# Self attention with 8-bit rounding: an input's scalings spread over two turns, new weights rounded behind the exponentials, output weights left unscaled

## The chip, the cores and the metric

One core of a Trainium2 chip runs the whole program. The metric is the device time of one execution in microseconds (us). Five runs of the kernel before gave a median of 3887.34 us (3884.24 to 3895.66). An engine is one of TensorE (PE, with its weight loads PEld), VectorE (DVE), ScalarE (ACT), GpSimd (POOL) and SyncE (SP, which here only issues DMAs). Each engine runs its own list of instructions in order; a semaphore holds an instruction until what it needs is done.

## What is computed

A decoder of two layers on 16 batches of 112 positions and 512 features. The change touches the second of its seven stages, the self-attention half of the first layer's mixed attention, and in one point the third, its cross-attention half. Cut to what matters:

```python
ln_out = _ln(hidden_states, ln_w, ln_b)
q = _ln(_fp8_linear_pertensor(ln_out, wq, wq_scale, q_in_scale).reshape(b, s, g, hpg, d), qln_w, qln_b)
k = _ln(_fp8_linear_pertensor(ln_out, wk, wk_scale, k_in_scale).reshape(b, s, g, d), kln_w, kln_b)
v = _fp8_linear_pertensor(ln_out, wv, wv_scale, v_in_scale).reshape(b, s, g, d)
core = _gqa(q, k, v).reshape(b, s, nh * d)
...
cat = jnp.concatenate([core, xout], axis=-1)
catq = _div_clamp_fp8(cat, proj_smooth)
return jnp.einsum('bsi,oi->bso', catq, wproj) * (proj_in_scale * proj_w_scale)
```

`_fp8_linear_pertensor` divides its input by a scale for each feature, rounds it to an 8-bit float and multiplies by the weights and both scales. The result of the last line is added to `x`.

## The kernel before

**Stages.** Seven stages follow each other. The first attends over the batch positions (up to about 290 us in the profile), the second is `stage_fp8_self` (L915, to about 960 us), the third `stage_fp8_cross` (to about 2310 us); then come a mixture of experts, another self attention, another cross attention and a feed-forward part.

**Units and turns.** The self stage has four head groups q of four heads each, and 16 batches. A unit (`SelfUnit`) is one (q, batch); `self_order` (L902) lists the 64 units: the eight batches 0 to 7 of q = 0 are units 0 to 7, then batches of q = 0 and q = 1 are mixed until unit 31, then q = 2 and q = 3 follow. The 16 x 112 rows make 14 tiles of 128 rows, so batches 7 and 15 have no tile of their own, and their units no query product. `turn(n)` (L956) runs n from -2 and works on several units at once: the query product, key and value products, and normalization of unit n; transposes of its normalized queries and keys one turn later; scores, minimum (`su_m`) and exponentials (`pr`) of unit n - 2; transposed probabilities (`pt`) and values (`ps_av`) of unit n - 3, followed by their division and rounding (`r_y`, `r_o`); the output product and its addition to `x` for unit n - 4. TensorE, ACT and, from turn 5 on, DVE run in exactly the order in which the code is written (`manual_schedule`, L1009 and L1012). POOL and SP are ordered by the scheduler's own estimate; it is fixed once the program is built.

**Inputs.** A unit of q = 0 with a tile makes its own input (`Quantized`): the normalized rows `xn` are loaded one turn ahead, transposed on TensorE into one PSUM bank (`ps_xt`), and scaled by ACT into 16 pieces `y` of 128 x 128, eight for queries and keys, four for values, four for the later cross stage (L695). `round_qk` and `round_v` round the first eight and the next four with `round_fp8`: four steps on DVE (L504 to L508) and a subtraction on POOL (L510), which writes `xq` or `xv`. Copies go to DRAM, from where the other head groups load them. In the kernel before, turn n does all of this for the input of unit n + 2. These inputs belong to units 0 to 6, 8, 10, 12, 15, 17, 19 and 22, so turns -2 to 4, 6, 8, 10, 13, 15, 17 and 20 carry one.

**Weights.** Each head group's weights arrive in 12 chunks of 128 x 512 (`raw`, two buffers), split by `Weights.part` (L597) into a rounded part `hi` and a remainder `lo`, so that two matmuls make one product (`two_parts`). Six chunks of the query and key weights are centered on DVE first (L587 to L594, at the end of the turn that loads them); at the start of the next turn `ends` runs: ACT casts to `hi` (L617), POOL subtracts (L618). Chunks that aren't centered, two of values and four of the output, are first scaled by ACT in place (L616), the values by the input's scales, the output by the one number `c_proj`. From turn 3 two chunks a turn are prepared for q = 1, from turn 24 two a turn for q = 2, from turn 31 one a turn for q = 3, and from turn 47 one a turn for the cross stage, which goes on in the same way itself.

**Statistics.** `project_kv` (L776) squares queries and keys on ACT (L761), sums on DVE (L764, `su_v`), and calls `rsqrt`, two POOL instructions (L491 and L492). `normalize` multiplies the products by it on DVE (L804, `qk`), which also frees their PSUM banks: the three banks `mm` hold query products (`ps_q`) and key and value products (`ps_kv`) in turn, the four banks `sc` hold scores, transposes, values and the output product.

**Early products.** In turns -2 to 4 TensorE also computes 16 key products of the cross stage (`ps_early`).

**Addition.** `add_output` (L894), called for each tile and head group by both the self and the cross stage, multiplies `r_o` by the output weights and adds the PSUM bank to `x` on DVE (L899).

## Time and profile before

| what | value |
| --- | --- |
| median of 5 runs | 3887.34 us (3884.24 to 3895.66) |
| the profiled execution's own time | 3887.62 us |
| its span, first to last instruction | 3885.9 us |
| mean granted clock of TensorE | 0.968 |
| TensorE busy, share of the span | 94% |
| VectorE, ScalarE, GpSimd | 45%, 38%, 24% |
| the 16 scalings of an input (L695), x224 | 537 ns mean of one, issued 0.37 us apart |
| cast of a chunk (L617), x48 and x32 | 619 and 618 ns (median) |
| scaling of an output chunk (L616), x32 | 731 ns (median) |
| scaling of half a value chunk (L616), x16 | 524 ns (median) |
| subtraction of a chunk on POOL (L618), x48 and x32 | 1286 and 1270 ns (median) |

The page gives busy time of each engine and the clock that the throttle granted. The span can be cut into stretches and busy time, clock and DMA share read for each; the table of waits says for which line an engine stood still and what released it, with the sum, the number and the longest; the timeline lists instructions in order of time with the idle time before them in brackets.

### The profile page before, as it was taken

To read this page: it belongs to the slowest core of one execution; us is meant where nothing else is said; L and a number is where in the kernel's file an instruction comes from. 1 tells how busy PE (TensorE), PEld (TensorE's weight loads), DVE (VectorE), ACT (ScalarE), POOL (GpSimd) and SP (SyncE) were. 2 spreads that over 40 slices of the span, in tenths; PEclk is the share of its full clock that TensorE was granted. 3 is DMA by queue.
4 is the path that set the end of the run, shared out by engine and by line. 5 is a ranking of instruction groups with operands and counts; after the bars stand their busy time and mean duration, and the time that the engine had idled before them with its cause. 6 is when DMAs were issued, how large, how long until landed. Compare 5 with 4: busy or idle time off the path is not lost.

```text
span 3885.9 us, 46312 instructions
## 1 busy us (share of the span) xinstructions
PE 3642.9 (94%) x16482; PEld 2353.8 (61%) x16482; DVE 1759.4 (45%) x3856; ACT 1462.5 (38%) x4189; POOL 935.1 (24%) x1322
## 2 busy tenths in 40 slices
PE   7888889999899999999999999999889989999999
PEld 4445778887555565666666654555444445556788
DVE  4445767775554544544445543111333343214333
ACT  2556666555544444444444430111123341112222
POOL 2333545554322322222222210000222220000000
PEclk8999889999999999999999999999989999999999
DMA  2125323442211211211121114999820013122000
GB/s 74 56 89 180 106 86 118 132 136 73 84 55 51 76 48 46 70 51 51 48 76 49 43 46 140 320 314 320 292 94 12 1 47 104 64 79 82 11 12 17
DMA packets 118118, 364.56 MB, mean 94 GB/s; under 512 B 13281, under 2 KB 33249, under 8 KB 108849
## 3 DMA queue, kind: packets, MB, share of 16 engines
q1 hardware_dynamic: 105504, 332.20, 26.5%
q0 software_dynamic: 5040, 16.52, 1.2%
q10 hardware_dynamic: 7344, 12.89, 0.9%
q8 instruction: 131, 2.15, 0.2%
q14 instruction: 99, 0.80, 0.1%
HBM read 317.09 MB, written 44.47 MB: 93 GB/s over the span
## 4 chain that ended last, share of the span: by engine, by line
PE 72%; DVE 7%; ACT 3%; issue 3%; POOL 3%; DMA 2%; SPq 0%; ACTq 0%; POOLq 0%; DVEq 0%
PE ps_kv L1081 14%; PE ps L1430 5%; PE ps_acc L664 4%; PE ps_q L664 4%; PE ps_av L1134 4%; PE ps_s L1109 3%; PE ps_y L1448 3%; PE ps_u L1785 3%; PE ps_o L341 3%; PE ps_o L1767 3%; PE ps_q L1536 3%; PE ps_g L1785 3%; PE ps_p L1629 3%; PE ps_pt L1124 2%; PE ps_kv L664 2%
## 5 line engine op out<-in xcount | busy, mean ns | idle before, releaser
L1081 PE MATMUL ps_kv<-w_kv,ct 128*125 128x512 f32 x1408 | 638.4, 593 | 0.0
L1081 PEld LDWEIGHTS ps_kv<-w_kv,ct 128*125 128x125 f32 x1408 | 261.4, 188 | 277.2 <-issue 242.0
L510 POOL TENSOR_TENSOR r_o<-r_t,r_m 128x64 fp32r<-128x64 bf16 (+6 forms) x224 | 146.6, 672 | 393.8 <-DVE r_t L508 369.7
L1025 ACT ACTIVATE pr<-ps_s,ex_m 112x375 f32<-112x375 f32 (+1 forms) x272 | 157.4, 579 | 161.1 <-DVE ex_m L1024 150.9
L1430 PE MATMUL ps<-w_expert,xgt 128*128 128x448 f32 x560 | 216.4, 539 | 0.7 <-ACT xgt L1422 0.7
L1057 DVE TENSOR_REDUCE cu_v<-sq 125x2 f32<-125x256 f32 (+1 forms) x248 | 118.6, 478 | 179.7 <-ACT sq L1056 179.5
L233 POOL TENSOR_TENSOR pr<-pr,nq_s 112x448 f32<-112x448 f32 (+1 forms) x120 | 119.4, 996 | 324.5 <-DVE nq_s L232 249.9
L492 POOL TENSOR_TENSOR cu_v<-cu_v,mhalf 125x2 f32<-125x2 f32 (+1 forms) x248 | 190.0, 766 | 20.6
L228 ACT ACTIVATE pr<-ps_s,nq_m 112x112 f32<-112x112 f32 (+1 forms) x480 | 167.3, 373 | 59.2 <-DVE nq_m L220 54.7
L491 POOL TENSOR_SCALAR cu_v<-cu_v 125x2 f32<-125x2 f32 (+1 forms) x248 | 48.0, 194 | 578.4 <-DVE cu_v L1057 575.7
L1109 PE MATMUL ps_s<-kt,qt 128*112 128x375 f32 x512 | 183.1, 479 | 1.4 <-ACT pr L1025 0.9
L1024 DVE TENSOR_REDUCE ex_m<-ps_s 112x1 f32<-112x375 f32 (+1 forms) x272 | 148.4, 545 | 69.1 <-PE ps_s L1656 67.5
L1056 ACT ACTIVATE sq<-ps_kv 125x256 f32<-125x256 f32 x176 | 67.4, 383 | 274.1 <-PE ps_kv L1081 221.5
L485 ACT ACTIVATE qt<-ps_t,turned 128x448 f32<-128x448 f32 (+6 forms) x224 | 116.3, 580 | 137.9 <-PE ps_t L1093 126.5
L1134 PE MATMUL ps_av<-pt,vn 125*128 125x224 f32 x768 | 163.3, 363 | 0.0
L1430 PEld LDWEIGHTS ps<-w_expert,xgt 128*128 128x128 f32 x560 | 103.6, 190 | 92.0 <-issue 91.0
L1124 PEld LDWEIGHTS ps_pt<-ident,pr 112*125 112x125 f32 x768 | 104.3, 191 | 89.1 <-DVE pr L1116 49.8
L242 ACT COPY ptt<-ps_pt 112x448 f32<-112x448 f32 (+1 forms) x120 | 67.3, 561 | 227.6 <-PE ps_pt L240 227.6
L1134 PEld LDWEIGHTS ps_av<-pt,vn 125*128 125x128 f32 x768 | 146.2, 195 | 8.6 <-ACT pt L1127 3.8
L1109 PEld LDWEIGHTS ps_s<-kt,qt 128*112 128x112 f32 x512 | 90.1, 177 | 99.9 <-issue 59.3
L1124 PE MATMUL ps_pt<-ident,pr 112*125 112x112 f32 x768 | 120.1, 287 | 31.5 <-DVE pr L1116 29.5
L485 ACT ACTIVATE kt<-ps_t,vec 128x375 f32<-128x375 f32 (+7 forms) x240 | 131.2, 587 | 26.6 <-PE ps_t L1099 22.5
(294 smaller groups left out, 7425.1 us busy)
## 6 DMA issues: line engine op xcount, KB each, us to landing
w_expert<-in_moe_w SPq DMA_DIRECT2D x105, 896.0 KB
ct<-in_ctx_t SPq DMA_DIRECT2D x64, 750.0 KB
xq<-xq_dram SPq DMA_DIRECT2D x42, 512.0 KB
xq<-xx_dram SPq DMA_DIRECT2D x56, 256.0 KB
raw<-in_self_w SPq DMA_DIRECT2D x48, 256.0 KB
w_sum<-in_ffn_w SPq DMA_DIRECT2D x12, 1024.0 KB
cn<-in_ctx SPq DMA_DIRECT2D x16, 750.0 KB
xv<-xv_dram SPq DMA_DIRECT2D x48, 224.0 KB
```

The source lines that it names most:

```text
L228: nc.scalar.activation(pr[:, j, :], self.ps[:, j, r * t : (r + 1) * t], AF.Exp, bias=self.mx[r][:, j : j + 1], scale=-1.0, accum_out=sums[ ...
L485: k.nc.scalar.activation(dst, src, AF.Identity, bias=cols[:, 1:2], scale=cols[:, 0:1])
L492: nc.gpsimd.tensor_tensor(dst, dst, bc(k.minus_half[: dst.shape[0]], [dst.shape[0], n]), ALU.pow)
L664: k.nc.tensor.matmul(out, lhs(c), w[i][:, c, :], start=first and c == 0 and i == 0, stop=last and c == n - 1 and i == 1,)
L1024: nc.vector.tensor_reduce(mx, src, AX.X, ALU.min)
L1025: nc.scalar.activation(dst, src, AF.Exp, bias=mx, scale=-1.0, accum_out=sums)
L1081: nc.tensor.matmul(pkv, self.ct[:, c, ch * CC : (ch + 1) * CC], w[:, c, :], start=c == 0, stop=c == KC - 1,)
L1109: nc.tensor.matmul(ps, self.heads.qt[self.b][:, h, :], self.kt[:, h // 2, :], start=True, stop=True)
L1124: nc.tensor.transpose(ps[:, h, :], self.pr[:, h, ch * CC : (ch + 1) * CC], k.ident[:S, :S])
L1134: nc.tensor.matmul(av[:, 2 * g : 2 * g + 2, :], self.vn[:, ch, g, :], self.pt[:, ch, 2 * g : 2 * g + 2, :], start=ch == 0, stop=ch == NCH - 1,
L1430: nc.tensor.matmul(pp, self.xt[:, c, :], w[:, c, :], start=c == 0, stop=c == 3)
L1785: nc.tensor.matmul(pp, w[:, c, cols], xt[:, part, c, :], start=c == 0 and part == 0, stop=c == 3 and part == 1,)
```

## The change

Three things are edited, all below.

First, an input is worked on over two turns. `new` is still the input of unit n + 2, but in turn n it is now only transposed and scaled ten times, at the turn's end. `half` is the input of unit n + 1: behind the exponentials its queries and keys are rounded, and six more scalings follow; its values are rounded behind the normalization. `xq` of unit n + 1 is thus made in turn n instead of turn n - 1.

Second, `ends` of all weights moves from the start of the turn to behind the exponentials. For the value weights the scaling and the cast become one ACT instruction for each 256 columns, and the remainder is made on DVE by `scalar_tensor_tensor` (raw times scale, minus `hi`) instead of on POOL.

Third, output weights are no longer scaled. Their factor `c_proj` goes into the addition, which becomes a `scalar_tensor_tensor` (product times `c_proj`, plus `x`), in the self and in the cross stage.

```diff
-        col = lambda i: k.c_proj if scale is None else k.w_cols[:, scale + i : scale + i + 1]
+        col = lambda i: k.w_cols[:, scale + i : scale + i + 1]
...
         def end():
             hi, lo = self.hi[n][:, cols], self.lo[n][:, cols]
-            if not centered:
-                for i in rows:
-                    part = raw[:, i * width - first : (i + 1) * width - first]
-                    nc.scalar.activation(part, part, AF.Copy, scale=col(i))
-            nc.scalar.copy(hi, raw)
-            nc.gpsimd.tensor_tensor(lo, raw, hi.bitcast(F32), ALU.subtract)
+            if centered or scale is None:
+                nc.scalar.copy(hi, raw)
+                nc.gpsimd.tensor_tensor(lo, raw, hi.bitcast(F32), ALU.subtract)
+                return
+            for i in rows:
+                part = slice(i * width - first, (i + 1) * width - first)
+                nc.scalar.activation(hi[:, part], raw[:, part], AF.Copy, scale=col(i))
+                nc.vector.scalar_tensor_tensor(
+                    lo[:, part], raw[:, part], col(i), hi[:, part].bitcast(F32),
+                    ALU.mult, ALU.subtract,
+                )
...
     two_parts(k, acc, lambda h: o[:, h, :], w)
-    k.nc.vector.tensor_tensor(k.x[:, t, :], k.x[:, t, :], acc, ALU.add)
+    x = k.x[:, t, :]
+    k.nc.vector.scalar_tensor_tensor(x, acc, k.c_proj, x, ALU.mult, ALU.add)
...
         def turn(n):
-            new = inputs.get(n + 2)
-            for w in weights:
-                w.ends()
+            new, half = inputs.get(n + 2), inputs.get(n + 1)
             products(early.get(n, 0))
...
             if at(n):
                 units[n].query_sums()
-            if new:
-                new.transpose()
             if at(n - 3):
                 units[n - 3].transpose_probs()
             if at(n - 2):
                 units[n - 2].exponentials()
-            if new:
-                new.scale(5)
+            if half:
+                half.round_qk()
+                xq[n + 1] = half.xq
+            for w in weights:
+                w.ends()
+            if half:
+                half.scale(6)
             if at(n):
                 units[n].project_kv(xv[order[n][0]].pop(order[n][1]))
             for w, count, pieces in due(n):
                 w.begin(count, pieces)
-            if new:
-                new.scale(5)
-                new.round_qk()
             if at(n - 3):
                 units[n - 3].values()
             if at(n):
                 units[n].normalize()
+            if half:
+                half.round_v()
             if at(n - 1):
                 units[n - 1].transpose()
             if at(n - 4):
                 units[n - 4].output()
             if new:
-                new.scale(6)
-                new.round_v()
-                xq[n + 2] = new.xq
+                new.transpose()
+                new.scale(10)
             elif at(n + 2):
```

## The prediction

> **What bounds the kernel now.** The page's first part and the clock row come first, then a table by stretches, cut where the stages and the kinds of turn change (columns: stretch; its us; busy us and instructions of PE, weight loads, DVE, ACT, POOL; granted clock; DMA share; GB/s).
>
> ```profile
> PE 3642.9 (94%) x16482; PEld 2353.8 (61%) x16482; DVE 1759.4 (45%) x3856; ACT 1462.5 (38%) x4189; POOL 935.1 (24%) x1322
> PEclk8999889999999999999999999999989999999999
> ```
>
> ```profile
> 300.00:380.00 80.00, 77.71 (x324) 48.40 (x324) 52.22 (x94) 51.71 (x154) 32.16 (x31) 0.98 0.54 180
> 380.00:429.00 49.00, 31.49 (x142) 26.52 (x142) 36.48 (x74) 31.00 (x93) 27.26 (x29) 0.72 0.34 110
> 452.00:476.00 24.00, 20.95 (x119) 18.47 (x118) 17.14 (x39) 15.53 (x51) 12.90 (x15) 0.86 0.33 113
> 600.00:640.00 40.00, 31.44 (x195) 27.62 (x194) 30.61 (x65) 20.83 (x69) 21.88 (x22) 0.96 0.34 103
> 960.00:2310.00 1350.00, 1310.33 (x4981) 816.04 (x4980) 673.95 (x1622) 598.06 (x1425) 346.37 (x646) 0.99 0.18 57
> ```
>
> TensorE sets the time nearly everywhere. The changed stage, about 290 to 960 us, is the exception: from 380 to 640 TensorE idles and its clock drops, and no other engine is full there, so chains of waits between engines rule. Until 380 the early key products cover everything. The cross stage (960 to 2310) is 97% TensorE. The waits of TensorE in 280:530, then one pair of turns of an input from the timeline, name the chain:
>
> ```profile
> PE ps_kv L664 <- DVE qk L804: 14.2, 5, 4.0
> PE ps_av L858 <- ACT pt L852: 10.2, 3, 5.2
> PE ps_s L826 <- ACT kt L485: 7.2, 5, 3.9
> ```
>
> ```profile
> 456.68 0.36 ACT L839 ACTIVATE pr<-ps_s,su_m 112x112 f32<-112x112 f32 x1
> ...
> 460.23 1.94 ACT L695 ACTIVATE y<-ps_xt,q_bias,q_gain 128x128 bf16<-128x128 f32 x5
> ...
> 463.72 2.12 POOL L510 TENSOR_TENSOR xq<-r_t,r_m 128x1024 fp32r<-128x1024 bf16 x1 [1.28 <-PE ps_q L664]
> 464.15 1.82 DVE L504 TENSOR_SCALAR r_y<-r_y 128x448 bf16<-128x448 bf16 x1
> ...
> 467.68 2.07 PE L664 MATMUL ps_kv<-w_self,xq 128*128 128x256 f32 x8 [2.70 <-DVE qk L804]
> ```
>
> Turn 10 starts at 452.57 (its ps_q), turn 11 at 461.19, turn 12 at 475.46: 22.9 us for a pair whose first turn scales an input. DVE runs in a fixed order, and its four rounding steps stand ahead of the normalization, so they wait for ACT's eighth scaling; then r_y (0.28 elsewhere) lies 1.82 beside POOL's xq. The keys of turn 11 wait for that, and the next 16 matmuls take 3.78 instead of 1.88, at half clock.
>
> The second kind of turn prepares weights (here two chunks a turn):
>
> ```profile
> 617.27 0.61 DVE L832 TENSOR_REDUCE su_m<-ps_s 112x4 f32<-112x448 f32 x1
> 617.38 0.62 ACT L617 CAST w_self<-raw 128x512 fp32r<-128x512 f32 x1 [1.92 <-DVE raw L594]
> 618.08 1.27 POOL L618 TENSOR_TENSOR w_self<-raw,w_self 128x512 fp32r<-128x512 f32 x1 [1.27 <-ACT w_self L617]
> 618.40 0.52 ACT L852 COPY pt<-ps_pt 112x448 f32<-112x448 f32 x1
> 618.81 0.37 ACT L839 ACTIVATE pr<-ps_s,su_m 112x112 f32<-112x112 f32 x1
> 618.97 1.03 PE L858 MATMUL ps_av<-pt,v 112*128 112x224 f32 x4 [3.85 <-ACT pt L852]
> ...
> 621.53 0.20 POOL L491 TENSOR_SCALAR su_v<-su_v 128x6 f32<-128x6 f32 x1
> ...
> 629.78 0.62 DVE L832 TENSOR_REDUCE su_m<-ps_s 112x4 f32<-112x448 f32 x1
> ```
>
> The visible wait is TensorE on pt, behind the cast, behind DVE's centering. But the turn's length, 12.5 us, is a ring: su_m, exponentials, squares of the keys, su_v on POOL, normalization, centering, su_m. Removing the visible wait doesn't shorten the ring.
>
> **Part 1, scalings over two turns.** The 16 scalings are all still there (1.87 for five, 0.37 each), as are the rounding steps. Ten scalings now stand at a turn's end; the query rounding stands behind the next turn's exponentials, six scalings follow, the value rounding stands behind the normalization. In the built program POOL does pr, xq, su_v in the second turn (before: pr, su_v, xq), so su_v queues behind 2.1 us of xq. Recomputed for turns 11 and 12, from the start of turn 11: ten scalings to 3.8, square 0.5, pt 0.4, exponentials 1.3 to 6.1; reciprocal 0.2; rounding 2.1, of which the first step lies beside pr, as one at 426.75 took 0.85 there instead of 0.27, so 0.7 more: 9.2; xq 2.1 and a hand-over: 11.6. The queries of turn 12 need this xq. TensorE is done at 8.5 and waits about 3.1, a wait that isn't there now. Turn 12: ps_q at half clock 3.6 (to 15.2), scores and pt 1.2, keys and values 1.9 (their xv, behind norm at 14.2, rounding 15.6 and POOL 1.3, is there by 17.0, before the second half), av, transposes, output 3.1, input transposes 0.35: 21.8. Before 22.9, so 1.1 a pair; six pairs (turns 9-10, 11-12, 14-15, 16-17, 18-19, 21-22): 6.6 less. Bounds: 15 less, if xq arrives in time and a pair falls to 19.3, near TensorE's own 8.4 a turn; 3 more, if one further collision of 1.6 with POOL falls in each.
> A rule is weighed here. The row says that 2.70 us of idling cost the 16 matmuls half their clock. The Trainium skill, TensorE: Matmul & The Clock Gate, Part 1, says the array goes cold after an idle window of about 3.4 us and then needs about 3.4 us of work. By the rule a 3.1 us wait could leave ps_q at full speed, and the pair, then waiting for xv, would be 21.6, an estimate that takes 1.2 off the six pairs; I follow the row.
>
> Turns 5 to 8 mix inputs and weights, 378.05 to 429.27. The raw chunks of turn 4 now load behind that turn's exponentials and, on SP's queue, behind an xv store: issued near 384 instead of 378.05, landed after the row's 5 us near 389 instead of 383.2. DVE waits there with normalization behind it. From then on ACT no longer sits behind casts that wait for centering (TensorE's 5.21 and 3.47 on pt) and the rounding doesn't wait for scalings. Followed as above, ps_q of turn 8 comes near 426: 3 less. Bounds: 8 less (the load isn't late), 4 more (the lateness is paid twice).
>
> The moved steps' stores (yx, xq, xv) go to SP a turn later; their readers are the next head groups, from turn 9 on, with turns to spare, and the xn load keeps its place behind the transposes, one turn ahead of use: nothing, but 2.1 where a load is late (TensorE waited 4.2 on xn in two places).
>
> Turns up to 4 and the first stage: nothing; matmuls of the early products cover the former (2.3 idle in 300:380). If that cover were gone, one scaling batch, 3.7, would show. The first stage keeps its TensorE order; bounds 2 either way for four short DVE steps.
>
> **Part 2, rounding behind the exponentials.** Centered chunks keep cast 0.62 and POOL 1.27 each. Gain: exponentials start 0.06 after su_m instead of 0.93, and centering no longer lies beside POOL's 1.27 (one step 1.64 instead of 0.75). Loss: the built POOL order is pr, chunks, su_v; before, chunks, pr, su_v. From the exponentials' end (618.81 and four steps of 0.33, so 620.14) su_v starts 1.39 later now, at 621.53; after: 0.49 + 0.93 + 2 x 1.27 = 3.96. The ring: su_m 0.68, exponentials 1.33, 3.96, su_v and hand-over 1.64, normalization to centering 1.53, centering 3.3 = 12.4, against 11.6 and 12.5 measured, the latter with the longer centering of 256-column chunks, for which it is 13.6. Over turns 25 to 28 with the tail of turns 29 and 30: 4.5 more (bounds 0 to 7). One chunk a turn: 9.5 against 9.09 (684.87 to 693.96), ten such turns: 4 more (bounds 0 to 6).
> The value weights' remainder goes from POOL to DVE, four steps of 0.48 a pair of chunks, in place of 2 x 1.27: no centering follows, so it lies beside TensorE's 8.4. If exposed, 2 each time.
>
> **Part 3, output weights.** ACT loses 32 scalings of 0.73; those in the self stage stood at a turn's start ahead of pt, and with the short waits at 717 to 760 I take 2 less (bounds 0 to 5). In the cross stage the same wait for pr (1.3) stands in turns with and without them, so nothing. The addition becomes a scalar_tensor_tensor of the same shape as L1802:
>
> ```profile
> L899 DVE TENSOR_TENSOR x<-x,ps_acc x112: 676/681/690, 402.8 to 2302.1; 128x512 f32<-128x512 f32 x112
> L1802 DVE SCALAR_TENSOR_TENSOR xo<-ps_o,t_s,x x14: 742/743/751, 3641.2 to 3882.2; 128x512 f32<-128x512 f32 x14
> ```
>
> 0.06 more, 112 times, 7 us of DVE beside TensorE; nobody waits for x. Bounds 0 to 2.
>
> **Sum.** -6.6 - 3 + 4.5 + 4 - 2 = -3.1 on the profiled 3887.62 (span 3885.9): 3884.5; the median of the runs is 0.3 lower, so 3884.
>
> **Rivals.** (a) *Gain outweighs:* POOL isn't what holds the second turn, and the six pairs come to 19.3, 15 less; turns 5 to 8 give 5; the rings lose 3. For it: no engine is over 75% busy from 380 to 429. Against: POOL's order as built. 3887 - 17 = 3870. (b) *The ring, slower:* su_v behind chunks and xq on POOL lengthens every such turn: 7 + 6 in the weight turns, 4 in turns 5 to 8, pairs unchanged, 3 back from ACT: 14 more, 3901. It decides as soon as the pairs give under 0.3 each. For it: the ring of measured rows. Against: TensorE's waits on pt, 10.2, 10.5 and 9.0 us in 280:530, 530:700 and 700:960, are real stalls. (c) *A wait takes the place of the old one, balanced:* the sum above, ps_q on xq instead of ps_kv on qk.
>
> **How the numbers follow.** 0.2% is 7.8 us, about what a measurement tells from no change. (c) 0.40, (a) 0.36, (b) 0.24; I give the three signs the same chances. The time is (c)'s, its own range 3878 to 3893. The bounds together reach further; 3860 holds most of (a), 3902 most of (b).
>
> **What would show it.** Right: TensorE waiting for POOL xq ahead of ps_q in turns 10, 12, 15; POOL L491 about 4 us after the exponentials in turns 25 to 27, su_m to su_m 12 to 14 there; no wait on pt. Part 3: the addition at 0.74, the stretch 960:2310 within 2 us. Wrong: ps_q of turn 23 (586.79 now) more than 15 or less than 2 us earlier, or 600:640 shorter than now.

## The result, and the profile after

The changed kernel takes 3903.64 us (median of 52 runs, 3894.11 to 3933.95), the kernel before 3889.1 us (median of 93, 3877.14 to 3914.87). The ratio is 1.0035, 95% interval 1.0027 to 1.0043: slower by 14 us. The forecast was 3884, with 3901 for the rival "the ring, slower".

The profiled execution has a span of 3899.6 us (before 3885.9). Its page, first the busy times, then the granted clock:

```profile
PE 3636.5 (93%) x16482; PEld 2343.3 (60%) x16482; DVE 1781.0 (46%) x3872; ACT 1440.0 (37%) x4149; POOL 925.6 (24%) x1314
...
PEclk8999899999999999999999999999999999999999
```

DVE has 21.6 us more to do than before (112 longer additions and 16 new steps make about 15 of it), ACT 22.5 less, TensorE the same work in 6.4 us less busy time. No total says that the kernel is slower. The stretches, with the columns of the table before (stretch; its us; busy us and instructions of PE, weight loads, DVE, ACT, POOL; granted clock; DMA share; GB/s):

```profile
300.00:380.00 80.00, 73.52 (x280) 43.34 (x281) 42.55 (x88) 44.95 (x132) 28.38 (x27) 0.96 0.53 169
380.00:429.00 49.00, 33.61 (x189) 28.84 (x187) 38.05 (x73) 33.53 (x106) 24.92 (x28) 0.86 0.32 100
452.00:476.00 24.00, 19.36 (x112) 17.00 (x112) 17.24 (x36) 15.41 (x51) 11.60 (x13) 0.86 0.35 115
600.00:640.00 40.00, 30.24 (x163) 26.48 (x162) 30.11 (x62) 19.18 (x64) 19.03 (x20) 0.84 0.36 110
960.00:2310.00 1350.00, 1310.03 (x4972) 815.47 (x4972) 675.69 (x1616) 589.51 (x1409) 347.10 (x641) 0.99 0.18 56
```

The cross stage (last line) has TensorE at 1310.03 us as before (1310.33), so the loss is elsewhere. 300:380, which the early products had covered, fell from 77.71 to 73.52 us of TensorE; 380:429 rose from 31.49 to 33.61; 600:640 fell from 31.44 to 30.24. To see where the time went, the starts of the query products (`ps_q`) of the two kernels were set against each other, from turn 0 to the first one of the cross stage, and the stage cut at turns 4, 8, 23 and 32. The first row is in us; the others are differences from it, each worked out from the start times in that kernel's own timeline:

| kernel | 0 to 4 | 4 to 8 | 8 to 23 | 23 to 32 | 32 to cross | sum |
| --- | --- | --- | --- | --- | --- | --- |
| before | 53.8 | 58.3 | 157.5 | 77.3 | 290.2 | 637.1 |
| changed | +5.6 | -5.0 | -6.0 | +8.9 | +8.3 | +11.8 |
| forecast, by the same cuts | 0 | -3 | -6.6 | +4.5 | +4 - 2 | -3.1 |

Before turn 0 the changed kernel is 0.7 later and behind the first cross product another 1.1, which makes the 13.7 between the spans. So turns up to 23 gave 5.4 us where 9.6 were forecast, and the weights' turns behind them cost 17.2 where 6.5 were forecast.

TensorE's waits in 280:530 (engine, line, tile and what released it; us in total, times, longest):

```profile
PE ps_q L669 <- POOL xq L510: 20.1, 6, 5.1
PE ps_xt L154 <- ACT y L700: 4.8, 5, 2.2
PE ps_kv L669 <- DVE qk L809: 4.3, 2, 3.7
```

The 14.2 us on `qk` and the 10.2 on `pt` of before are down to 4.3 and 2.7; the wait on `xq` ahead of `ps_q` has come, in turns 10, 12, 15 and others, as forecast (5.14 us in turn 10, 2.77 to 2.83 in turns 12, 15, 17 and 19). The line on `ps_xt` is new: it isn't one that the prediction had.

In 700:960, the same view:

```profile
PE ps_acc L669 <- ACT pr L844: 10.8, 4, 3.1
PE ps_s L831 <- ACT kt L485: 4.6, 3, 2.2
```

The 9.0 us on `pt` are down to 1.4, but the output product waits 10.8 instead of 4.9 for a PSUM bank that late exponentials (`pr`) give back, and 4.6 us on `kt` are new.

The turns that prepare weights, in the timeline of the changed kernel (start, us, engine, line, operation, outputs and inputs; in brackets the idle time before and what ended it), turns 27 and 28; TensorE is a turn ahead, so its score products here are those of turn 28:

```profile
626.40 0.62 DVE L837 TENSOR_REDUCE su_m<-ps_s 112x4 f32<-112x448 f32 x1
...
627.12 0.35 ACT L844 ACTIVATE pr<-ps_s,su_m 112x112 f32<-112x112 f32 x1 [6.43 <-DVE su_m L837]
...
628.45 1.14 ACT L614 CAST w_self<-raw 128x512 fp32r<-128x512 f32 x2
...
629.48 0.40 ACT L766 ACTIVATE sq<-ps_kv 128x256 f32<-128x256 f32 x1
...
629.82 2.49 POOL L615 TENSOR_TENSOR w_self<-raw,w_self 128x512 fp32r<-128x512 f32 x2
629.91 0.42 DVE L769 TENSOR_REDUCE su_v<-sq 128x2 f32<-128x256 f32 x1 [1.13 <-ACT sq L766]
...
630.92 0.85 ACT L485 ACTIVATE kt<-ps_t,vec 128x160 f32<-128x160 f32 x2
...
631.49 1.84 PE L831 MATMUL ps_s<-kt,qt 128*112 128x112 f32 x8 [4.96 <-ACT kt L485]
...
632.28 0.22 POOL L491 TENSOR_SCALAR su_v<-su_v 128x6 f32<-128x6 f32 x1
...
633.97 0.69 DVE L809 TENSOR_TENSOR qk<-ps_q,su_v 128x512 f32<-128x512 f32 x1 [0.47 <-POOL su_v L492]
...
634.90 0.61 DVE L837 TENSOR_REDUCE su_m<-ps_s 112x4 f32<-112x448 f32 x1
...
636.95 1.70 ACT L619 ACTIVATE w_self<-raw,w_cols 128x256 fp32r<-128x256 f32 x4
...
637.50 2.33 DVE L620 SCALAR_TENSOR_TENSOR w_self<-raw,w_cols,w_self 128x256 fp32r<-128x256 f32 x4 [0.22 <-ACT w_self L619]
...
638.54 0.38 ACT L766 ACTIVATE sq<-ps_kv 128x256 f32<-128x256 f32 x1
...
640.24 0.21 POOL L491 TENSOR_SCALAR su_v<-su_v 128x6 f32<-128x6 f32 x1 [1.89 <-DVE su_v L769]
```

Read it from the exponentials (627.12, four of them, done at 628.48). Behind them ACT runs the two casts first (1.14), so the keys' squares start at 629.48; POOL takes the two subtractions (2.49) ahead of `su_v`, which starts at 632.28, 3.8 behind the exponentials; normalization follows at 633.97, and only then the next `su_m`. In the kernel before su_v started 1.39 behind the exponentials. From su_m to su_m this turn takes 8.50 us, before 6.84. In the next turn it is value weights: ACT spends 1.70 and DVE 2.33 on them before the squares at 638.54 are summed, and su_v comes at 640.24. TensorE meanwhile has run ahead and stands 4.96 us at `kt`, and its eight score products then take 1.84 instead of 0.95.

The addition measures as forecast, 0.74 to 0.75 (count; minimum, median and maximum in ns; first and last start):

```profile
L905 DVE SCALAR_TENSOR_TENSOR x<-ps_acc,c_proj,x x112: 742/745/753, 408.6 to 2314.4; 128x512 f32<-128x512 f32 x112
```

### The profile page after: what moved, and what is told of

The parts are those of the page before. It is cut to its first block, busy times and chain, and to the rows that moved or that the text cites. A ratio compares the mean times of both kernels' runs of the same rounds, so it can differ in the third digit from the quotient of the medians.

```text
span 3899.6 us, 46275 instructions
## 1 busy us (share of the span) xinstructions
PE 3636.5 (93%) x16482; PEld 2343.3 (60%) x16482; DVE 1781.0 (46%) x3872; ACT 1440.0 (37%) x4149; POOL 925.6 (24%) x1314
## 4 chain that ended last, share of the span: by engine, by line
PE 72%; DVE 8%; POOL 4%; ACT 3%; issue 3%; DMA 2%; SPq 0%; POOLq 0%; ACTq 0%; DVEq 0%
PE ps_kv L1086 14%; PE ps L1435 5%; PE ps_q L669 4%; PE ps_av L1139 4%; PE ps_acc L669 3%; PE ps_s L1114 3%; PE ps_y L1453 3%; PE ps_u L1790 3%; PE ps_o L341 3%; PE ps_q L1541 3%; PE ps_o L1772 3%; PE ps_g L1790 3%; PE ps_p L1634 3%; PE ps_pt L1129 2%; PE ps_v L1556 1%
## 5 line engine op out<-in xcount | busy, mean ns | idle before, releaser
L492 POOL TENSOR_TENSOR cu_v<-cu_v,mhalf 125x2 f32<-125x2 f32 (+1 forms) x248 | 190.3, 767 | 20.5
L669 PE MATMUL ps_acc<-w_self,r_o 128*128 128x512 f32 x448 | 123.5, 420 | 27.5 <-ACT pr L844 15.7
```

The lines of the kernel that those rows point to most:

```text
L492: nc.gpsimd.tensor_tensor(dst, dst, bc(k.minus_half[: dst.shape[0]], [dst.shape[0], n]), ALU.pow)
L669: k.nc.tensor.matmul(out, lhs(c), w[i][:, c, :], start=first and c == 0 and i == 0, stop=last and c == n - 1 and i == 1,)
```

## The experiments

All lengths below are from the `ps_q` of turn 0 to the first `ps_q` of the cross stage ("the stage", before 637.1), in one profiled execution each; ratios are of timed runs on the same chip, with their 95% interval. The kernel before itself, profiled a second time, gave 635.6.

> The kernel before, unchanged, profiled once more: how far its own self stage moves between executions. If the profile of before is typical: first cross ps_q within 2 us of 954.2 and clock 0.97. If executions differ in the clock of turns 6 to 12: some us apart there and the same from turn 13 on.

Turn 0 came 4.5 us later there, and between turns 46 and 52 1.4 were won; in the rest of the stage the two executions agree within 0.4. Two other kernels below, profiled twice, differ by 4.0 and 6.9 in the stage, nearly all of it before turn 23. So a single difference of under 7 us before turn 23, or of under 2 behind it, is weighed as nothing here; what is read before turn 23 rests on differences that come again in several kernels. The timed runs are also less favourable than the stage: by their medians 16 of the 17 comparisons with the kernel before stand 1 to 12 us worse than the stage lengths do, 4 in the middle. Why stays open, so a stage that is under some 5 us shorter is no proof of a faster kernel.

**Each part alone.** Three kernels carry one part each. The first has the inputs over two turns and nothing else (the weights' `ends` stay at the turn's start):

```diff
-            new = inputs.get(n + 2)
+            new, half = inputs.get(n + 2), inputs.get(n + 1)
             for w in weights:
                 w.ends()
...
+            if half:
+                half.round_qk()
+                xq[n + 1] = half.xq
+                half.scale(6)
```

> The kernel before with part 1 alone (the scalings over two turns); weights rounded at the turn's start, output weights as before. Theory 'places': the loss of 5 us in turns 2 to 4 (TensorE's input transposes wait for the one tr bank, ps_xt on ACT y) and the gain of the six pairs in turns 9 to 22 both belong to this part: ps_q of turn 4 near 377 (before 370.9), then 7 to 10 us won back by turn 23, nothing lost behind it; in all -2 against before (bounds -5 to +2). Rival 'weights on DVE' (the loss is the value weights' remainder on DVE): the same here. Rival 'shared gain' (the gain in turns 5 to 23 comes from the weights behind the exponentials): ps_q of turn 23 about 5 us later than before, +5.

Measured: stage 627.4, that is 9.7 less; ratio 0.9982 (0.9966 to 0.9997). Turn 23 came 8.5 earlier counted from turn 0. The part is a gain and not a loss, and the rival "shared gain" falls: the pairs don't need the rounding behind the exponentials. The expected size was off, -9.7 instead of -2.

The second moves `ends` only:

```diff
-            for w in weights:
-                w.ends()
             products(early.get(n, 0))
...
                 units[n - 2].exponentials()
+            for w in weights:
+                w.ends()
```

> The kernel before with the weights' rounding moved behind the exponentials and nothing else: inputs in one turn, output and value weights scaled by ACT and subtracted on POOL as before. Theory 'places': turns 2 to 4 as before (ps_q of turn 4 within 1 us of 370.9), some 3 us won in turns 25 to 27, 9 lost in the turn whose ends are value weights behind the centering of key chunks (turn 28), 4 lost at turns 30 to 32 and 8 lost behind 700 us: +10 to +18 against before, with TensorE waits on kt in place of those on pt. Rival 'weights on DVE': the value remainder is on POOL here, so the losses don't show: -4 to +2.

Measured: stage 654.8, 17.8 more; ratio 1.0066 (1.0041 to 1.0092). Turns 28 to 29 took 18.0 us (before 9.3) and TensorE waited 4.89 on kt there, with the value weights' remainder on POOL. So the rival that blames DVE's new steps falls, and the move alone costs more than the whole change.

The third has the new rounding code and the addition, with `ends` at the turn's start:

```diff
-            nc.scalar.copy(hi, raw)
-            nc.gpsimd.tensor_tensor(lo, raw, hi.bitcast(F32), ALU.subtract)
+            if centered or scale is None:
...
+                nc.vector.scalar_tensor_tensor(
+                    lo[:, part], raw[:, part], col(i), hi[:, part].bitcast(F32),
...
-    k.nc.vector.tensor_tensor(k.x[:, t, :], k.x[:, t, :], acc, ALU.add)
+    k.nc.vector.scalar_tensor_tensor(x, acc, k.c_proj, x, ALU.mult, ALU.add)
```

> The kernel before with the new rounding code (value weights scaled on ACT straight into the high part, remainder by a DVE step; output weights unscaled) and the factor in the addition, but rounded at the turn's start as before, inputs in one turn. Theory 'places': -4 to 0 against before, turn 28 as before. Rival 'weights on DVE': the losses are here: +9 in turn 28, +5 to +10 in all. The addition 0.74 instead of 0.68; 960 to 2310 within 2 us by both.

Measured: stage 641.6, 4.6 more; ratio 1.0038 (1.0022 to 1.0054); turns 28 to 29 took 9.5. Neither theory is met: no gain, and not the loss in turn 28 either. The two halves of this part were then run apart. Output weights unscaled with the factor in the addition, alone:

```diff
-            if not centered:
+            if not centered and scale is not None:
                 for i in rows:
```

> The kernel before with the output weights unscaled and the factor in the addition, nothing else (value weights scaled on ACT and subtracted on POOL as before). Theory 'value weights' (of the 4.6 us that the new rounding code and the addition together lost between the first self and the first cross ps_q, all lie in the turns that end value weights, where their DVE steps stand ahead of the other work): 636 to 637 us between these two marks (before 637.1), 0 to -3 in all. Rival 'addition' (the longer addition or the missing scalings cost): 639 or more, and 960 to 2310 longer by over 2 us.

Measured: stage 637.6, 0.5 more; ratio 1.0011 (0.9998 to 1.0025). ACT's saved scalings win nothing, and the longer addition loses nothing that can be told.

The value weights' new steps alone (the same code as above, for chunks with a scale that aren't centered):

> The kernel before with the value weights' new rounding alone (ACT scales straight into the high part, the remainder is two DVE steps of 0.48 a chunk), at the turn's start; output weights and addition as before. Theory 'value weights': 641 us between the first self and the first cross ps_q (before 637.1), the loss in turns 6 to 8 (+2.3) and 38 to 40 (+3.0); +4 to +5 in all. Rival 'addition': 637.

Measured: stage 638.1, 1.0 more; ratio 1.0010 (1.0000 to 1.0020). Both theories miss: the halves give 1.5 together, the whole gave 4.6. The timed ratios do add (1.0011 and 1.0010 against 1.0038, with intervals of 0.001 and more). Whether the whole part loses more than its halves or the 4.6 is scatter stays open; it isn't the loss that was looked for.

Set beside the changed kernel, the three parts alone add up to it in the profiles, stretch by stretch:

| kernel | 0 to 4 | 4 to 8 | 8 to 23 | 23 to 32 | 32 to cross | sum |
| --- | --- | --- | --- | --- | --- | --- |
| inputs over two turns | +5.5 | -4.3 | -9.7 | +0.7 | -1.9 | -9.7 |
| rounding moved | -0.1 | -2.6 | +1.9 | +8.5 | +10.1 | +17.8 |
| new rounding code, addition | -0.9 | +2.0 | +0.9 | +0.6 | +2.0 | +4.6 |
| sum of the three | +4.5 | -4.9 | -6.9 | +9.8 | +10.2 | +12.7 |
| changed | +5.6 | -5.0 | -6.0 | +8.9 | +8.3 | +11.8 |

The timed ratios add less well: 0.18% less, 0.66% and 0.38% more make 0.86% more, where the changed kernel has 0.35%. That stays open.

**The changed kernel without the move.** All parts, `ends` back at the turn's start:

> The changed kernel with the weights' rounding back at the turn's start; parts 1 and 3 and the new rounding code stay. Theory 'places' (the parts act by their own places, the move alone cost 17 us at the first cross turn, part 1 won 10, the rest lost 3): first cross ps_q near 954.2 - 10.3 + 2.7 = 946.6, against 966.8 in the changed kernel, turn 28 to 29 about 9 us instead of 18.4; in all -8 to -4 against before (3877). Rival 'interplay' (part 1 and the new code together bring the loss, whatever the place of the rounding): 955 or later, no better than before.

Measured: stage 633.0, 4.1 less than before; turns 28 to 29 took 9.4; ratio 1.000 (0.998 to 1.002). The loss behind turn 23 is gone (+0.9 and +1.2), so it belongs to the move. The sum came out 2 us worse than expected, and the timed runs show no gain over the kernel before.

**The turns up to 4.** The changed kernel's new wait on `ps_xt`, in its timeline (turns 2 and 3):

```profile
351.39 2.22 ACT L700 ACTIVATE y<-ps_xt,q_bias,q_gain 128x128 bf16<-128x128 f32 x6
...
353.66 0.69 PE L154 MATMUL ps_xt<-ident,xn 128*128 128x128 f32 x4 [2.21 <-ACT y L700]
...
354.15 8.73 PE L658 MATMUL ps_early<-w_kv,w_ct 128*125 128x512 f32 x16
...
362.31 2.44 PE L669 MATMUL ps_q<-w_self,xq 128*128 128x512 f32 x8
```

The input transposes now stand at a turn's end and write the one bank of `ps_xt`, which the last of the previous input's six scalings frees at 353.6; TensorE waits 2.21, and the 16 early products behind it take 8.73 us instead of 7.03. Done in one turn, the transposes found that bank free. So the inputs 0 to 6 were put back into one turn, in the changed kernel and in the kernel with the inputs' part alone:

```diff
+            one = n < 5
+            half = None if one or n == 5 else half
...
+            if new and one:
+                new.transpose()
```

> The changed kernel with the inputs of turns 0 to 6 done in one turn as before, two turns only from input 8 on. Theory 'places': ps_q of turn 4 within 1 us of 370.9 instead of 377.2, the waits of ps_xt on ACT y gone, and 5 us less at the end: 3898 or +10 against before. Rival 'cover': the early products would give the 5 us back anyway by turn 8 (where the changed kernel is only 1.3 late): 0 to 1.5 less at the end.

> The kernel before with the scalings over two turns for the inputs from input 8 on only; inputs 0 to 6 in one turn, weights and output weights as before. Theory 'places': the 5 us of turns 2 to 4 aren't lost and the rest of part 1's gain stays: ps_q of turn 23 13 to 14 us earlier than before, first cross ps_q near 939 (before 954.2, part 1 alone 944.0), 3865 to 3870. Rival 'cover': turn 5 to 8 gives back what turns 2 to 4 lost, so no more than part 1 alone: 943 to 945.

Measured: in the changed kernel the stage fell from 648.9 to 641.8, and turns 0 to 4 from +5.6 to -0.1; ratio to before 1.0036 (1.0019 to 1.0053), while its profile ended 8.5 us ahead of the changed kernel's. In the kernel with the inputs' part alone: stage 625.8 against 627.4, ratio 0.9983 (0.9969 to 0.9996) against 0.9982. The 5.5 us in turns 0 to 4 stand in all four profiled kernels that spread the early inputs, and in no other. Without the moved rounding turns 4 to 8 give nearly all of them back (-4.3 with, +0.2 without); "cover" is right there. Beside the moved rounding the profile gives none back, but the timed runs don't bear this out: 1.0036 is no better than the changed kernel's 1.0035. In both kernels inputs from 8 on give the whole gain of 8 to 23.

**One step further back.** If casts and subtractions between the exponentials and su_v are what costs, they should cost little behind su_v. The kernel before, with `ends` behind `project_kv`, which holds the keys' squares, the value copy and su_v:

```diff
                 units[n].project_kv(xv[order[n][0]].pop(order[n][1]))
+            for w in weights:
+                w.ends()
```

> The kernel before with the weights' rounding moved behind the keys' squares, the value copy and su_v (one step further back than behind the exponentials). Theory 'queue' (behind the exponentials ACT's casts of 1.1 to 3.0 us hold the keys' squares and POOL's chunks of 2.5 hold su_v): su_v starts 1.3 to 1.5 behind the exponentials' end in turns 27 to 29 instead of 3.8, only kt stays 1 to 3 us later; from the first self to the first cross ps_q 640 to 646, between before (637.1) and behind the exponentials (654.8). Rival 'raw buffers' (what costs is that the next chunks' loads start later and centering waits): later still than behind the exponentials, 655 or more.

Measured: stage 628.7, which is 8.4 less than before and 26.1 less than with the same work one step earlier; ratio 1.000 (0.998 to 1.002). This is lower than either theory gave. Its timeline in turn 27 (columns as above; the score products are those of turn 28):

```profile
628.66 0.62 DVE L832 TENSOR_REDUCE su_m<-ps_s 112x4 f32<-112x448 f32 x1
...
630.70 0.39 ACT L761 ACTIVATE sq<-ps_kv 128x256 f32<-128x256 f32 x1
...
631.22 1.17 ACT L617 CAST w_self<-raw 128x512 fp32r<-128x512 f32 x2
...
632.08 0.20 POOL L491 TENSOR_SCALAR su_v<-su_v 128x6 f32<-128x6 f32 x1
...
633.65 2.50 POOL L618 TENSOR_TENSOR w_self<-raw,w_self 128x512 fp32r<-128x512 f32 x2
633.72 0.69 DVE L804 TENSOR_TENSOR qk<-ps_q,su_v 128x512 f32<-128x512 f32 x1 [0.26 <-POOL su_v L492]
...
633.75 1.84 PE L826 MATMUL ps_s<-kt,qt 128*112 128x112 f32 x8 [4.28 <-ACT kt L485]
...
635.62 0.62 DVE L832 TENSOR_REDUCE su_m<-ps_s 112x4 f32<-112x448 f32 x1 [0.88 <-PE ps_s L826]
```

The squares follow the exponentials at once (630.70), su_v comes 1.35 behind their end at 630.73, normalization at 633.72, and the subtractions lie behind su_v. From su_m to su_m it is 6.96, where the changed kernel takes 8.50. TensorE's wait on kt is still there, 4.28, with half clock behind it: the most visible new wait of these turns was not what made the changed kernel slower.

The same one move in the changed kernel:

> The changed kernel with one move: the weights' rounding stands behind the keys' squares, the value copy and su_v instead of behind the exponentials; all else as changed. Theory 'queue' (what made the changed kernel slower is that its casts and chunks stand between the exponentials and su_v): from the first self to the first cross ps_q 648.9 less about 26 = 623 (628 at most), su_v 1.3 to 1.5 us behind the exponentials in turns 27 to 29, TensorE's wait on kt of 4 to 5 us in turn 28 still there; 8 to 14 less than before at the end. Rival 'kt' (the wait of TensorE on kt with half clock behind it is the loss, as the casts delay kt): kt stays late here, so 645 or more and no faster than before.

Measured: stage 624.7, 24.2 less than the changed kernel and 12.3 less than before; the wait on kt in turn 28 is 3.26 and su_v comes 1.35 behind the exponentials. The rival "kt" falls. Counted from su_m to su_m (us), the turns behind 23 show where the move helps and where it doesn't:

| kernel | turns 25 to 27, with centering | turns 27 to 31, without |
| --- | --- | --- |
| before | 24.1 | 30.1 |
| before, all behind the exponentials | 26.1 | 37.7 |
| before, all behind su_v | 26.2 | 32.6 |
| changed | 26.2 | 37.8 |
| changed, all behind su_v | 26.0 | 30.9 |

Of the 7.6 us that the changed kernel loses in turns 27 to 31 the one move takes back 6.9. The 2 us in the two centering turns are lost in both places. Behind su_v something else holds these turns: su_v is early, but DVE waits for the next chunks to be centered, a wait that the kernel before and the changed one don't have there. In the kernel before with all behind su_v:

```profile
611.57 0.69 DVE L587 TENSOR_REDUCE w_mean<-raw 128x4 f32<-128x512 f32 x1 [2.41 <-DMA raw<-in_self_w]
```

The two `raw` buffers come free only after the subtractions: these start at 607.48, and the first load is issued at 608.78, as the first of them ends. So in the centering turns the rival "raw buffers" is right, though its forecast for the whole stage, 655 or more, isn't.

The ratio is 0.9984 (0.9963 to 1.0005), less than the stage promises; the profiled execution shows one reason, TensorE's waits among the experts, far behind the change:

```profile
PE ps L1435 <- DMA w_expert<-in_moe_w: 14.2, 15, 2.7
```

The expert part (from the first to the last group of expert products) took 377.7 us there, against 359.6 in the changed kernel and in the kernel before. One other execution showed that (below); what sets it off stays open.

**ACT's casts or POOL's subtractions?** The kernel before with ACT's work behind the exponentials and POOL's behind su_v:

```diff
-            nc.gpsimd.tensor_tensor(lo, raw, hi.bitcast(F32), ALU.subtract)
+            return lambda: nc.gpsimd.tensor_tensor(lo, raw, hi.bitcast(F32), ALU.subtract)
...
+            rest = [r for w in weights for r in w.ends()]
...
+            for r in rest:
+                r()
```

> The kernel before with ACT's casts and scalings of weights behind the exponentials (as in the run with the rounding alone moved there) but POOL's subtraction behind su_v. Theory 'POOL' (its chunks of 2.5 ahead of su_v are most of the loss): 630 to 636 from the first self to the first cross ps_q, near the run with all behind the squares (628.7). Theory 'ACT' (the casts ahead of the keys' squares are most of it): 645 to 655, near the run with all behind the exponentials (654.8). A share of both: in between.

Measured: stage 653.2, ratio 1.0048 (1.0027 to 1.0069). It tells nothing apart: POOL isn't in the list of engines with a fixed order, and in the timeline its subtractions still stand ahead of su_v (633.32 and 635.77 in turn 27). With POOL added to that list its order is the one that was meant:

```diff
-        with k.tc.manual_schedule(engines=fixed | {mybir.EngineType.DVE}):
+        with k.tc.manual_schedule(engines=fixed | {mybir.EngineType.DVE, mybir.EngineType.Pool}):
```

> As the run with ACT's casts alone behind the exponentials, but with POOL's order fixed to that of the program, so that its subtractions now do stand behind su_v (in the run before this one the scheduler had put them ahead of it again, and nothing was told apart). Theory 'POOL' (its chunks of 2.5 ahead of su_v are most of the loss): 630 to 636 from the first self to the first cross ps_q. Theory 'ACT' (the casts and scalings of 1.1 to 3.0 ahead of the keys' squares are most of it): 645 to 655. A share of both: in between.

Measured: stage 648.1, ratio 1.0051 (1.0033 to 1.0069), in turns 27 and 28:

```profile
639.24 0.62 DVE L833 TENSOR_REDUCE su_m<-ps_s 112x4 f32<-112x448 f32 x1
...
641.29 1.15 ACT L618 CAST w_self<-raw 128x512 fp32r<-128x512 f32 x2
...
642.31 0.40 ACT L762 ACTIVATE sq<-ps_kv 128x256 f32<-128x256 f32 x1
...
643.26 0.21 POOL L491 TENSOR_SCALAR su_v<-su_v 128x6 f32<-128x6 f32 x1 [0.56 <-DVE su_v L765]
...
644.84 2.60 POOL L619 TENSOR_TENSOR w_self<-raw,w_self 128x512 fp32r<-128x512 f32 x2
...
649.00 0.91 ACT L617 ACTIVATE raw<-raw,w_cols 128x256 f32<-128x256 f32 x2 [0.16 <-DMA raw<-in_self_w]
...
651.96 0.38 ACT L762 ACTIVATE sq<-ps_kv 128x256 f32<-128x256 f32 x1
...
652.88 0.21 POOL L491 TENSOR_SCALAR su_v<-su_v 128x6 f32<-128x6 f32 x1 [2.75 <-DVE su_v L765]
```

Here su_v waits for no subtraction (643.26, the subtractions at 644.84), yet with value weights (from 649.00) it still comes 4.1 behind the exponentials, because ACT's scalings and casts, 3.1 us with the old code, stand ahead of the squares at 651.96. By stretches:

| kernel | 8 to 23 | 23 to 32 | 32 to cross | sum of the stage |
| --- | --- | --- | --- | --- |
| all behind the exponentials | +1.9 | +8.5 | +10.1 | +17.8 |
| only ACT's work there | +4.4 | +8.8 | -3.1 | +11.0 |
| all behind su_v | -0.7 | +3.8 | -11.7 | -8.4 |

The sum lies in the range of the theory "ACT". The stretches show a share of both. From 32 on, with one chunk a turn, 13.2 of the 21.8 us between the first and the last row go with POOL's place and 8.6 with ACT's. From 23 to 32 the equal +8.5 and +8.8 don't mean that POOL's part is nothing: turns 27 to 28 fall from 8.49 to 6.97 from su_m to su_m, so there it was all POOL's; turns 28 to 31 take 28.97, against 29.16 with all behind the exponentials and 25.62 with all behind su_v, so there nearly all is ACT's. And the two centering turns get longer, 28.0 instead of 26.1, with DVE waiting 2.40, 0.37 and 2.37 for raw chunks. What POOL's fixed order costs by itself was not run, and the 4.4 us in 8 to 23 aren't traced, so the shares are no more than a first split.

**Ahead of the exponentials, and the best version.** The rounding between the copy of pt and the exponentials, with inputs from 8 on over two turns:

> As the run with inputs from 8 on, with the weights' rounding between the copy of pt and the exponentials. Theory 'behind the exponentials is what costs' (there ACT's casts stand ahead of the keys' squares and POOL's chunks ahead of su_v; ahead of the exponentials they lie in the wait for su_m): no loss at turns 28 to 29 (about 9 us), no wait of TensorE on kt over 2 us there, and the waits on pt behind the casts (5.6 us in 560:620, 5.4 in 670:720, 3.8 in 810:860 before) gone; first cross ps_q 0 to 10 us earlier than with the rounding at the start. Rival 'any later place is late' (the raw buffers come free later, so loads and centering move): 5 us or more later than with the rounding at the start.

> The kernel with inputs from 8 on over two turns and the rounding between pt and the exponentials once more, on another chip: its profile gave 621.8 us from the first self to the first cross ps_q (15 less than before), its timed runs only 2 to 4 less. If the profiled execution was typical: 622 again and a ratio near 0.996. If executions differ in the self stage: another length in this profile, and the ratio again near 0.999 to 1.000.

Measured: turns 28 to 29 took 13.2 and 13.0, not the 9 expected, as `ps_q` of turn 28 comes earlier there (turns 23 to 32 together +2.9 and +2.7); stage 621.8 and 625.8, ratios 0.9996 (0.998 to 1.0012) and 0.9979 (0.9964 to 0.9993), so 0 to 4 us better in the stage than with the rounding at the turn's start (625.8), and not to be told apart in the runs. The rival "any later place is late" falls. TensorE's waits on pt from 590 to 960 us fell from 18.3 (rounding at the turn's start) to 2.0, but the output product now waits 19.0 instead of 5.1 behind late exponentials: the wait has moved. In the second profile the expert part took 378.0 us, which hid the gain of the stage in that execution.

Inputs from 8 on over two turns and the rounding behind su_v, with the old rounding code and addition:

> The kernel before with inputs from 8 on over two turns and the rounding behind the keys' squares and su_v (rounding code, output weights and addition as before). If the gains add: 637.1 - 11.3 - 8.4 = 617 from the first self to the first cross ps_q, and a ratio of 0.994 to 0.997, the best of all. If both take the same idle time: 624 to 628, 0.998.

> The kernel with inputs from 8 on over two turns and the rounding behind the keys' squares once more, to narrow its interval (0.9941 to 0.9986): 615 to 617 us from the first self to the first cross ps_q again, ratio 0.994 to 0.998. Rival: the first profile was a lucky one, 620 or more and 0.998 to 1.000.

Measured: stage 615.4 and 622.3; 3867.78 us, ratio 0.9963 (0.9941 to 0.9986), and on another chip 3865.92 us, ratio 0.9956 (0.9941 to 0.9970). The first stage length is near what the two gains add up to (617), the second is what the rival gave (620 or more), with 6.7 of the 6.9 us between them before turn 23; both ratios lie where the gains add. This version beats the kernel before by 16 to 18 us in the runs beside it, and by the ratios (0.9963 and 0.9956 against 1.0035) the changed one by an estimated 28 to 31.

## Why the prediction was wrong

- **What bounds the kernel**: right. The self stage is ruled by chains between engines; the cross stage didn't change (1354.4 us from its first query product to the first product of the shared expert, 1355.4 after).
- **Turns up to 4, "nothing, the early products cover the former"**: wrong, +5.6. The step looked only at ACT's scalings. The transposes moved as well, and they share one PSUM bank with the previous input. The price it gave for a lost cover, 3.7, is two thirds of that.
- **Turns 5 to 8, -3**: -5.0. A gain was right; how it comes about was not tested step by step, and part of it may be the 5.6 given back.
- **Six pairs, -6.6**: -6.0, and -9.7 for the inputs' part alone. The wait is as written: in four of the six pairs the queries wait 2.77 to 2.83 for xq where 3.1 were forecast, and in turn 12 `ps_q` at half clock takes 3.64 where 3.6 were forecast. That the sum fits is in part luck. It sets turns 11 and 12 after (21.8) against turns 10 and 11 before (22.9); turns 11 and 12 took 20.5 before and 19.1 after, as turn 12 has no output product and no input transposes, which the sum counts. And the pairs are unlike: turns 9 and 10 lost 1.4 with a wait of 5.14, the other five gained 1.2 to 3.4 each.
- **Rounding behind the exponentials, +4.5**: this is the step that failed. The ring of the centering turns is right: POOL's order is pr, chunks, su_v, su_v came 3.8 behind the exponentials (forecast 3.96), and from su_m to su_m turns 25 to 27 took 12.6 and 13.7 (forecast 12.4 and 13.6; before 11.6 and 12.5). But the prediction let the ring bind only where centering closes it, and held of the value weights' steps: "no centering follows, so it lies beside TensorE's 8.4". The turns without centering lost most, from su_m to su_m 1.7, 2.3, 1.2 and 2.5 us in turns 27 to 31, in sum 7.6 where the two centering turns lost 2.1; 23 to 32 cost 8.9. "If exposed, 2 each time" was the right price for the value turn (10.75 against 8.41). There ACT's 1.70 and DVE's 2.33 stand ahead of the keys' squares and their sum; the same steps behind su_v gave 9.25. The prediction counted POOL's queue and left ACT's out: with POOL's subtractions behind su_v turns 28 to 31 still took 28.97 (all behind the exponentials 29.16, before 23.3).
- **One chunk a turn, +4, and output weights, -2**: +8.3 in sum. A turn of keys measured 9.6 (forecast 9.5), but from su_m to su_m the key turns 32 to 37 lost only 1.9; the turns with the output weights of q = 3 (41 to 44) lost 2.6 and those with the cross weights (49 to 55) 4.2. The -2 was not there: unscaled output weights alone gave +0.5.
- **Addition, 0.06 each, hidden**: right, 0.74, and nobody waits for it for more than 1 us in all.
- **The signs**: xq ahead of `ps_q`, su_v about 4 us late, 12 to 14 us from su_m to su_m, the addition at 0.74 and the cross stage within 2 us all came, and of the waits on pt (29.7 us) 6.1 were left. They looked only at the turns that the sum had priced, and so could not show that it was wrong elsewhere.
- **The rivals**: "the ring, slower", 3901, is what happened, 3903.64. Its price for the weight turns, 7 + 6, was too low (17.2), and it missed the +5.6 in turns 2 to 4. It was held to be the least likely because TensorE's waits on pt, 10.2, 10.5 and 9.0, "are real stalls". They went, and the weight turns became longer: the chain that sets those turns ran through the exponentials, the squares and su_v, and into this chain the work was put. "Gain outweighs" is off by 34 us; its price for the pairs doesn't fit itself, as six pairs falling from 22.9 to 19.3 are 21.6 less, not 15.

## What to carry to other kernels

When work is moved out of an engine's wait, ask what stands between its new place and the next link of the chain. At the turn's start the stage took 637.1 us; behind the exponentials, where the work delays su_v (by 2.4 us in turn 27 of the changed kernel), 654.8; one step further back 628.7. Price every kind of turn: the turns that the prediction held to be covered lost more than those it had counted. Count the moved step on every engine that it touches (here ACT's casts as well as POOL's subtractions), ask what a later place holds back (here the buffers of the next chunks), and check which engines keep the written order before an order is argued from the code. A conspicuous new wait in a profile may be only a mark: the wait on kt stayed at 4.3 us in the version whose stage was 26 us shorter.

## What the runs showed of the hardware

The same wait of TensorE doesn't always cost its clock. Two query products of the changed kernel, each behind a wait of 2.77 us on the same step of POOL:

```profile
525.24 3.48 PE L669 MATMUL ps_q<-w_self,xq 128*128 128x512 f32 x8 [2.77 <-POOL xq L510]
...
546.41 2.13 PE L669 MATMUL ps_q<-w_self,xq 128*128 128x512 f32 x8 [2.77 <-POOL xq L510]
```

One takes 3.48 us at a granted clock of 0.57, the other 2.13 at 1.00. Of the changed kernel's four waits of 2.77 to 2.83 us ahead of `ps_q` three were followed by a slow product (3.40 to 3.64), and a wait of 2.98 in turn 8 was not (2.13). In all the kernels with inputs over two turns together, 54 such waits of 2.75 to 2.85 were followed by 3.3 us or more 32 times, by 2.2 or less 15 times and by something between 7 times. So a forecast that takes either answer for all turns is off by up to 1.5 us a turn.

The Trainium skill, TensorE: Matmul & The Clock Gate, Part 1, says that the window in which activity is judged runs freely and isn't set by when a kernel starts. The unequal rows agree with that, and no run here shows it by itself. The page also puts the idle window after which the array is cold at about 3.4 us; here pauses of 2.75 to 2.85 were often enough (32 of 54).

In two of the 19 profiled executions the expert part took 378 us instead of 360, with TensorE waiting for weights (14.2 and 13.6 us). The DMA engines' busy share doesn't tell them apart: 0.92 to 1.03 there from 2400 to 2750 us in steps of 50, and 0.95 to 1.02 in a run of 360. Both belong to kernels with a short self stage, but others as short don't show it; a gain of 12 us in one stage can be hidden by this in a single execution.
